# Two adder convolutions: four of nine taps' maxima summed in pairs by accumulating DMA

## The chip, the cores and the metric

The kernel runs on one core of one Trainium2 chip, in one launch. The metric is the device time in microseconds (us) of that core. A core has five engines that run side by side and meet at semaphores: TensorE (PE in the profile; PEld is its weight load), VectorE (DVE), ScalarE (ACT), GpSimd (POOL) and SyncE (SP). Sixteen DMA engines move data when an engine's queue issues a transfer.

## What is computed

The kernel is a chain of four small networks (layers 0 to 3) on one input of 4 images, 128 channels, 64 x 64 pixels, all in float32. The change touches layer 1 alone:

```python
def adder_conv(x, w):            # 3x3, stride 1, pad 1
    # p: [4, 128*9, 4096] patches of x; wf: [128, 128*9]
    # per output channel wc:
    return -jnp.sum(jnp.abs(p - wc[None, :, None]), axis=1)

out = adder_conv(shift_conv(x, w_shift1), w_add1)
out = relu(batchnorm(out, g1, b1))
out = adder_conv(shift_conv(out, w_shift2), w_add2)
out = batchnorm(out, g2, b2)          # then + x and relu
```

`shift_conv` is an ordinary 3x3 convolution whose weights are rounded to powers of two. An adder convolution has no product in it: for every output channel (128), image (4), tap (9), input channel (128) and pixel (4096) it takes |p - w|, and sums over taps and input channels. With 2 adder convolutions that is 2 x 4 x 128 = 1024 pairs of image and output channel; below, one such pair is called a channel.

## The kernel before

Layer 1 calls `shift_adder` twice (tags `a1` and `a2`), and all of the change lies in that function and in the two small loaders `plain` and `normed` of `layer1`. The image after the shift convolution stands in SBUF with a border of zeros as `pb` [128 input channels, 66, 66]; a tap is a shifted view of it. One channel is nine such views of 128 x 4096 elements, each compared with one weight per partition.

Two engines make the absolute values. ACT computes |p - w| directly (L423: ACTIVATE Abs with -w as bias, output tile `aa`). DVE uses |p - w| = 2 max(p, w) - p - w and computes only the maximum (L430: TENSOR_SCALAR, output `da`); the sums of p and of w over the taps that go by maxima are added once, from `sums_of_p` (L370) and `wsum`. PE sums over the 128 input channels: `gather` (L381) multiplies the tile by a 128 x 32 matrix `pick` that is -1 or -2 in column jj and zero elsewhere, so that channel jj's sum lands in row jj of a PSUM bank that collects 32 channels. A tile that PE gathers is called a stream here; it costs 8 matmuls of 128 x 512, and as they are float32 each shows as 2 instructions in the profile, 16 in all.

Before, a channel has eight streams. Taps 4, 5, 6 are Abs on ACT; taps 0 to 3 are maxima on DVE. Taps 7 and 8 share one stream: ACT computes |p - w|/2 of tap 7 (`HALF_TAP`), and DVE adds tap 8's maximum onto that tile (L434: SCALAR_TENSOR_TENSOR), which therefore waits for ACT. So ACT has 4 ACTIVATEs a channel, DVE 4 TENSOR_SCALARs and one SCALAR_TENSOR_TENSOR. In every fourth channel of images 0 to 2 (`extra`) DVE joins tap 3 to tap 2 by a second SCALAR_TENSOR_TENSOR, which takes one stream off PE, and three steps of other PE work are put in: `sums_of_p` and the shift convolution of the next image (L349, with copies to `pb` at L354; its input blocks come by SP's queue, L512 or L519, and their borders are cleared by POOL, L331 to L335). Every 32 channels a bank pair is evacuated (L391, L392) and stored (L394).

The scheduler of the framework orders each engine's instructions by priority; the tile pools set how far an engine may run ahead: `da` has 3 buffers, `aa` 4. POOL has almost nothing to do in this layer, and no DMA is issued from POOL's queue anywhere in the kernel.

Of the kernel before, what the change touches and what calls it, by code (L numbers as in the profile page):

```python
# [28 lines left out]

DVE_TAPS = (0, 1, 2, 3)  # L30
ACT_TAPS = (4, 5, 6)
HALF_TAP = 7
MAX_TAP = 8
# [248 lines left out]
def shift_adder(tc, cm, load, wqs, w_add, stats, y_d, tag):  # L282
# [5 lines left out]

    nc = tc.nc
    NC = P // 32  # L290
    with ExitStack() as ctx:
# [4 lines left out]
        for t, scale in [(HALF_TAP, -0.5)] + [(t, -1.0) for t in ACT_TAPS]:  # L296
            wn[t] = cp.tile([P, P], F32, name=f"{tag}wn{t}")
            nc.vector.tensor_scalar(wn[t], wa[:, t, :], scale, None, ALU.mult)

        pick = {}  # L300
        for v in (-1.0, -2.0):
            pick[v] = cp.tile([P, 63], F32, name=f"{tag}pick{int(-v)}")
            nc.vector.memset(pick[v], 0.0)
            nc.vector.memset(pick[v][:, 31:32], v)

        xin_pool = ctx.enter_context(tc.tile_pool(name=f"{tag}x", bufs=3))
        pb_pool = ctx.enter_context(tc.tile_pool(name=f"{tag}p", bufs=2))
        dp = ctx.enter_context(tc.tile_pool(name=f"{tag}d", bufs=3))
        ap = ctx.enter_context(tc.tile_pool(name=f"{tag}a", bufs=4))
# [6 lines left out]
        sum_taps = DVE_TAPS + (MAX_TAP,)  # L316
        pw = ps_c.tile([P, NC], F32, tag="cv", name=f"{tag}pw")
        for c in range(NC):
            for g in range(4):
                for i, t in enumerate(sum_taps):  # L320
                    nc.tensor.matmul(
                        pw[32 * g : 32 * g + 32, c : c + 1], wa[:, t, 32 * c : 32 * c + 32], cm.one_col,
                        start=(i == 0), stop=(i == len(sum_taps) - 1), skip_group_check=True,
                    )
# [3 lines left out]
        def fetch(b, k):  # L328

            t = xin_pool.tile([P, RB + 2, HP], F32, tag="xin", name=f"{tag}xin{b}_{k}")  # L330
            nc.gpsimd.memset(t[:, :, 0:HP:HP - 1], 0.0)  # L331
            if k == 0:
                nc.gpsimd.memset(t[:, 0, 1 : 1 + W], 0.0)
            if k == NB - 1:
                nc.gpsimd.memset(t[:, RB + 1, 1 : 1 + W], 0.0)  # L335
            lo, hi = max(RB * k - 1, 0), min(RB * (k + 1) + 1, H)
            at = lo - (RB * k - 1)
            load(b, lo, hi, t[:, at : at + hi - lo, 1 : 1 + W])
            return t

        def convolution(b, pb):

            xin = fetch(b, 0)
            for k in range(NB):
                here, xin = xin, fetch(b, k + 1) if k < NB - 1 else None
                pc = ps_c.tile([P, BK], F32, tag="cv", name=f"{tag}pc{b}_{k}")
                for t in range(TAPS):
                    y, x = divmod(t, 3)
                    nc.tensor.matmul(  # L349
                        pc, wqs[:, t, :], here[:, y : y + RB, x : x + W],  # L350
                        start=(t == 0), stop=(t == TAPS - 1),
                    )
                    if t == TAPS - 1:
                        nc.vector.tensor_copy(pb[:, 1 + RB * k : 1 + RB * (k + 1), 1 : 1 + W], rows(pc))  # L354
                    yield

        def padded(b):
            t = pb_pool.tile([P, HP, HP], F32, tag="pb", name=f"{tag}pb{b}")
            clear_border(nc, t)
            return t  # L360

        def sums_of_p(b, pb, sp):

            for k in range(2):
                pc = ps_c.tile([P, BK], F32, tag="cv", name=f"{tag}sp{b}_{k}")
                for i, t in enumerate(sum_taps):
                    y, x = divmod(t, 3)
                    for g in range(4):
                        r = RB * (4 * k + g) + y
                        nc.tensor.matmul(  # L370
                            pc[32 * g : 32 * g + 32, :], cm.ones[:, 0:32], pb[:, r : r + RB, x : x + W],
                            start=(i == 0), stop=(i == len(sum_taps) - 1), skip_group_check=True,
                        )
                    yield
                nc.vector.tensor_copy(sp[:, k, :], pc)

        def gather(pa, jj, v, d, first=False):

            for k in range(2):
                for g in range(4):  # L380
                    nc.tensor.matmul(  # L381
                        pa[k][32 * g : 32 * g + 32, :],
                        pick[v][:, 31 - jj : 63 - jj],
                        d[:, bass.ts(4 * k + g, BK)],
                        start=first, stop=False, skip_group_check=True,
                    )

        def evacuate(b, c, pa, sp):
            for k in range(2):
                o = ep.tile([P, BK], F32, tag="ev", name=f"{tag}ev{b}_{c}_{k}")  # L390
                nc.vector.scalar_tensor_tensor(o, pa[k], wsum[:, c : c + 1], sp[:, k, :], ALU.add, ALU.add)  # L391
                nc.vector.bn_stats(stats[:, c, 2 * b + k, :], o)  # L392
                to = y_d[b, 32 * c : 32 * c + 32, :].rearrange("j (k g w) -> k g j w", k=2, g=4)
                nc.sync.dma_start(to[k], o)  # L394
# [11 lines left out]
        done, late = None, []  # L406
        for b in range(B):
            pb = pb_of[b]

            def view(t):  # L410
                y, x = divmod(t, 3)
                return pb[:, y : y + H, x : x + W]

            sp_of[b] = sp_pool.tile([P, 2, BK], F32, tag="sp", bufs=2, name=f"{tag}sps{b}")
            steps = beside(b, pb_of)
            for co in range(P):
                c, jj = divmod(co, 32)
                name = f"{tag}_{b}_{co}_"

                def absolute(t):  # L420
                    at = ap.tile([P, N], F32, tag="ab", name=f"a{name}{t}")
                    half = t == HALF_TAP
                    nc.scalar.activation(  # L423
                        rows(at), view(t), AF.Abs, bias=wn[t][:, co : co + 1], scale=0.5 if half else 1.0
                    )
                    return at

                def maximum(t):
                    dt = dp.tile([P, N], F32, tag="ad", name=f"d{name}{t}")
                    nc.vector.tensor_scalar(rows(dt), view(t), wa[:, t, co : co + 1], None, ALU.max)  # L430
                    return dt

                def plus_maximum(at, t):
                    nc.vector.scalar_tensor_tensor(  # L434
                        rows(at), view(t), wa[:, t, co : co + 1], rows(at), ALU.max, ALU.add
                    )

                if jj == 0:
                    pa = [
                        ps_a.tile([P, BK], F32, tag=f"pa{k}", name=f"{tag}pa{b}_{c}_{k}") for k in range(2)  # L440
                    ]


                extra = b < B - 1 and co % 4 == 1
                ah = absolute(HALF_TAP)
                d = maximum(DVE_TAPS[0])
                for g in late:
                    gather(*g)
                gather(pa, jj, -2.0, d, first=(jj == 0))
                if done and jj == 0:  # L450
                    evacuate(*done)
                d = maximum(DVE_TAPS[1])
                gather(pa, jj, -2.0, d)
                a = absolute(ACT_TAPS[0])
                gather(pa, jj, -1.0, a)
                a = absolute(ACT_TAPS[1])
                plus_maximum(ah, MAX_TAP)
                gather(pa, jj, -2.0, ah)
                gather(pa, jj, -1.0, a)
                if extra or b == B - 1:  # L460
                    for _ in range(3 if extra else 1):
                        next(steps, None)
                d = maximum(DVE_TAPS[2])
                if extra:
                    plus_maximum(d, DVE_TAPS[3])
                    a = absolute(ACT_TAPS[2])
                    late = [(pa, jj, -1.0, a), (pa, jj, -2.0, d)]
                else:
                    gather(pa, jj, -2.0, d)
                    a = absolute(ACT_TAPS[2])  # L470
                    d = maximum(DVE_TAPS[3])
                    gather(pa, jj, -2.0, d)
                    late = [(pa, jj, -1.0, a)]
                if jj == 31:
                    done = (b, c, pa, sp_of[b])
            for _ in steps:
                pass
        for g in late:
            gather(*g)
        evacuate(*done)  # L480


@with_exitstack
def layer1(ctx, tc, cm, w_shift1, w_add1, g1, b1, w_shift2, w_add2, g2, b2, x1d, y1d, y2d, stats_d):
# [26 lines left out]
    def plain(b, lo, hi, t):  # L511
        nc.sync.dma_start(t, rows(x1d[b])[:, lo:hi, :])  # L512

# [4 lines left out]
    def normed(b, lo, hi, t):  # L518
        nc.sync.dma_start(t, rows(y1d[b])[:, lo:hi, :])  # L519
        nc.vector.tensor_scalar(t, t, mean1, sc1, ALU.subtract, ALU.mult)  # L520
        nc.scalar.activation(t, t, AF.Relu, bias=vec["b1"])
# [867 lines left out]
```

## Time and profile before

| | us |
|---|---|
| median of 3 runs (22255.7 to 22260.05) | 22259.76 |
| the profiled execution, its own time | 22268.93 |
| its span in the trace | 22267.1 |
| adder loop a1, first ACTIVATE to last gather | 2083.8 to 9551.9 |
| adder loop a2, first ACTIVATE to last gather | 9640.3 to 17115.3 |

| in the stretches 2095 to 9540 and 9655 to 17113 (eight windows, 14903 us in sum) | busy us | share |
|---|---|---|
| ACT | 14806.94 | 99% |
| PE | 14385.61 | 97% |
| DVE | 14337.48 | 96% |
| POOL | 28.63 | 0.2% |

The DMA share in these eight windows is 0.01. Outside the loops lie layer 0 (before 2084), the start of a2, and layers 2 and 3 (after 17115); the change does not touch layers 0, 2 and 3.

How to read it: the profile's page gives busy time per engine, a strip of the span in 40 slices, the chain of waits that ended last, and the costliest groups of instructions with their count, busy time and mean duration. Where instructions of one engine overlap slightly (the next begins before the last has ended), the busy time of a group divided by its count is a little under the mean duration.

### The profile page before, as it was taken

The page shows a single profiled execution, that of the slowest core. Times are in us where ns is not written, and L with a number is a line of the kernel's source. Part 1 is how long each engine was busy: PE and PEld are TensorE (multiplying, and loading weights), DVE is VectorE, ACT ScalarE, POOL GpSimd, SP SyncE. Part 2 cuts the span into 40 slices and gives each one's busy share as a digit, 9 for nine tenths or more (in the row PEclk, how much of TensorE's full clock was granted, in tenths as well). Part 3 has the DMA queues.
Part 4 walks back from the last instruction along what each step waited for, and adds up shares of the span by engine and source line. Part 5 has one row for each costly group of instructions (what it writes and reads, how often), then busy time and mean ns, then how long its engine had stood idle before and what let it go on. Part 6 is the DMA issues. An engine that isn't in the chain of part 4 may idle for free.

```text
span 22267.1 us, 326916 instructions
## 1 busy us (share of the span) xinstructions
PE 20221.7 (91%) x144108; PEld 6559.1 (29%) x144108; DVE 19731.7 (89%) x9928; ACT 18549.7 (83%) x9373; POOL 3775.5 (17%) x1774
## 2 busy tenths in 40 slices
PE   9998999999999999999999999999997657688887
PEld 4443222222222232222222222223222222223222
DVE  7887999999999999989999999999998666688887
ACT  5665999999999999989999999999998233556555
POOL 5663000000000000000000000000000000388887
PEclk9999999999999999999999999999998776799998
DMA  0000000000000000000000000000000001588887
GB/s 12 12 5 13 3 4 4 4 4 4 2 4 4 4 2 2 2 8 4 5 3 3 4 3 4 4 2 2 2 3 33 0 0 72 160 217 216 217 219 191
DMA packets 267494, 811.85 MB, mean 36 GB/s; under 512 B 119692, under 2 KB 120596, under 8 KB 195924
## 3 DMA queue, kind: packets, MB, share of 16 engines
q1 hardware_dynamic: 265492, 782.55, 12.8%
q8 instruction: 1127, 18.46, 0.3%
q10 hardware_dynamic: 576, 8.39, 0.1%
q14 instruction: 299, 2.45, 0.0%
HBM read 662.02 MB, written 128.78 MB: 36 GB/s over the span
## 4 chain that ended last, share of the span: by engine, by line
ACT 28%; PE 24%; DVE 23%; issue 16%; DMA 7%; POOL 1%; SPq 0%; DVEq 0%; ACTq 0%; POOLq 0%
ACT aa L423 27%; DVE da L430 11%; PE a1pa L381 5%; PE pe L154 4%; PE pav L197 4%; DMA dl<-delta_d 3%; PE a2pa L381 3%; DVE da L434 3%; DVE aa L434 3%; DMA du<-du_d 2%; DVE h L1043 2%; DVE g L713 1%; PE pd L698 1%; PE mg L1058 1%; POOL dbu L1022 1%
## 5 line engine op out<-in xcount | busy, mean ns | idle before, releaser
L423 ACT ACTIVATE aa<-a1pb,a1wn 128x4096 f32<-128x4096 f32 x2048 | 7411.9, 3711 | 179.0 <-DVE a1pb L354 130.4
L423 ACT ACTIVATE aa<-a2pb,a2wn 128x4096 f32<-128x4096 f32 x2048 | 7410.7, 3709 | 45.3 <-PE a2pa L381 41.5
L430 DVE TENSOR_SCALAR da<-a1pb,a1wa 128x4096 f32<-128x4096 f32 x1952 | 4470.8, 2349 | 0.7 <-PE a1pa L381 0.6
L430 DVE TENSOR_SCALAR da<-a2pb,a2wa 128x4096 f32<-128x4096 f32 x1952 | 4471.0, 2349 | 0.2
L381 PE MATMUL a2pa<-da,a2pick 128*32 128x512 f32 x31232 | 3617.3, 594 | 254.7 <-DVE da L430 252.0
L381 PE MATMUL a1pa<-da,a1pick 128*32 128x512 f32 x31232 | 3615.4, 594 | 253.6 <-DVE da L430 250.9
L381 PE MATMUL a2pa<-aa,a2pick 128*32 128x512 f32 x32768 | 3714.1, 593 | 4.8 <-ACT aa L423 3.3
L381 PE MATMUL a1pa<-aa,a1pick 128*32 128x512 f32 x32768 | 3712.8, 592 | 4.9 <-ACT aa L423 3.3
L434 DVE SCALAR_TENSOR_TENSOR aa<-a1pb,a1wa,aa 128x4096 f32<-128x4096 f32 x512 | 2295.6, 4484 | 281.8 <-ACT aa L423 277.0
L434 DVE SCALAR_TENSOR_TENSOR aa<-a2pb,a2wa,aa 128x4096 f32<-128x4096 f32 x512 | 2295.6, 4484 | 278.2 <-ACT aa L423 274.5
L1058 PE MATMUL mg<-h,ident 128*128 128x512 f32 x4096 | 2017.7, 638 | 421.6 <-ACT m L1067 386.3
L1043 DVE TENSOR_TENSOR_SCAN h<-da,h,dbu 128x1024 f32<-128x1024 f32 x768 | 1804.3, 2349 | 485.6 <-ACT da L1029 393.9
L381 PEld LDWEIGHTS a2pa<-aa,a2pick 128*32 128x32 f32 x32768 | 1068.7, 110 | 2465.4 <-issue 2396.6
L381 PEld LDWEIGHTS a1pa<-aa,a1pick 128*32 128x32 f32 x32768 | 1068.7, 110 | 2463.8 <-issue 2399.3
L381 PEld LDWEIGHTS a2pa<-da,a2pick 128*32 128x32 f32 x31232 | 986.6, 110 | 2707.5 <-issue 2053.9
L381 PEld LDWEIGHTS a1pa<-da,a1pick 128*32 128x32 f32 x31232 | 986.7, 110 | 2705.5 <-issue 2053.7
L1058 PEld LDWEIGHTS mg<-h,ident 128*128 128x128 f32 x4096 | 785.7, 202 | 1658.5 <-issue 809.2
L191 POOL TENSOR_TENSOR ssum<-ssum,et 128x512 f32<-128x512 f32 x960 | 1228.8, 1280 | 233.3 <-ACT et L186 166.4
L1022 POOL TENSOR_TENSOR dbu<-du,B 128x2048 f32<-128x2048 f32 x256 | 1157.2, 4532 | 341.8 <-DMA du<-du_d 267.9
L1071 POOL TENSOR_TENSOR m<-m,C 128x2048 f32<-128x2048 f32 x256 | 1156.1, 4527 | 224.2 <-ACT m L1067 213.4
L1029 ACT ACTIVATE da<-dl,af 128x1024 f32<-128x1024 f32 x512 | 572.9, 1119 | 689.9 <-DMA dl<-delta_d 442.3
L156 ACT COPY et<-pe 128x512 f32<-128x512 f32 x1024 | 596.5, 583 | 591.4 <-PE pe L154 574.8
(273 smaller groups left out, 14087.9 us busy)
## 6 DMA issues: line engine op xcount, KB each, us to landing
dl<-delta_d SPq DMA_DIRECT2D x256, 512.0 KB
dl<-delta_d SPq DMA_DIRECT2D x512, 256.0 KB
du<-du_d SPq DMA_DIRECT2D x256, 512.0 KB
du<-du_d SPq DMA_DIRECT2D x512, 256.0 KB
xs_d<-xs SPq DMA_DIRECT2D x8, 2048.0 KB
sz_d<-sz SPq DMA_DIRECT2D x64, 256.0 KB
delta_d<-dv SPq DMA_DIRECT2D x32, 512.0 KB
du_d<-du SPq DMA_DIRECT2D x32, 512.0 KB
```

The costliest lines, as they stand in the source:

```text
L154: nc.tensor.matmul(pe, k[:, bass.ts(j, P)], unit[u, "q"], start=True, stop=True)
L156: nc.scalar.copy(et, pe)
L191: nc.gpsimd.tensor_tensor(unit[u, "sum"], unit[u, "sum"], at, ALU.add)
L197: nc.tensor.matmul(unit[u, "av"], image[u // NB][2][:, j, :], at, start=(j == 0), stop=(j == NJ - 1))
L381: nc.tensor.matmul(pa[k][32 * g : 32 * g + 32, :], pick[v][:, 31 - jj : 63 - jj], d[:, bass.ts(4 * k + g, BK)], start=first, stop=False, s ...
L423: nc.scalar.activation(rows(at), view(t), AF.Abs, bias=wn[t][:, co : co + 1], scale=0.5 if half else 1.0)
L430: nc.vector.tensor_scalar(rows(dt), view(t), wa[:, t, co : co + 1], None, ALU.max)
L434: nc.vector.scalar_tensor_tensor(rows(at), view(t), wa[:, t, co : co + 1], rows(at), ALU.max, ALU.add)
L1022: then(nc.gpsimd.tensor_tensor(t, du, by_states(tiles[n][0], 0, h), ALU.mult))
L1043: then(nc.vector.tensor_tensor_scan(t[:, cols][:, s], da[:, s], st[n, "dbu", h][:, cols][:, s], 0.0 if e % 4 == 0 else st["last"], ALU.mul ...
L1058: then(nc.tensor.matmul(pm, cm.ident, st[n, way, h][:, bass.ts(k, BK)], start=(way == 0), stop=(way == 1)))
L1071: then(nc.gpsimd.tensor_tensor(m, m, by_states(tiles[n][0], 1, h), ALU.mult))
```

## The change

Taps are dealt out anew, into seven streams. `PAIR_TAPS` ((0,1),(2,3)): DVE computes the maxima of both taps of a pair into two tiles, in halves of 128 x 2048 (`pair`, L455 of the new file), and a DMA issued from POOL's queue adds the first half tile onto the second, SBUF to SBUF (`accum_op=ALU.add`, L457); PE then gathers the sum once. That is four such DMAs of 1 MiB a channel, 4096 in the kernel. Tap 4 is a maximum on DVE (L446), taps 6, 7, 8 are Abs on ACT (L441), and tap 5 (`EITHER_TAP`) is Abs on ACT in even channels and a maximum on DVE in odd ones. The half tiles have 8 buffers (the pairs of one channel), the whole maxima 1, the Abs tiles 3. The combined half-and-maximum stream and the `extra` channels' second SCALAR_TENSOR_TENSOR are gone.

Nearly every instruction of the function is wrapped in `then(...)` (`tc.keep_in_program_order`), so each engine keeps the order in which the code names it: a channel's pairs are gathered one channel later, as the listing shows. The input blocks of a shift convolution are fetched two ahead instead of one, and the normalisation in `normed` is issued when the block is used.

```diff
-DVE_TAPS = (0, 1, 2, 3)
-ACT_TAPS = (4, 5, 6)
-HALF_TAP = 7
-MAX_TAP = 8
+PAIR_TAPS = ((0, 1), (2, 3))
+MAX_TAP = 4
+EITHER_TAP = 5
+ACT_TAPS = (6, 7, 8)
...
-        dp = ctx.enter_context(tc.tile_pool(name=f"{tag}d", bufs=3))
-        ap = ctx.enter_context(tc.tile_pool(name=f"{tag}a", bufs=4))
+        mp = ctx.enter_context(tc.tile_pool(name=f"{tag}m", bufs=8))
+        dp = ctx.enter_context(tc.tile_pool(name=f"{tag}d", bufs=1))
+        ap = ctx.enter_context(tc.tile_pool(name=f"{tag}a", bufs=3))
...
+            ahead = [fetch(b, 0), fetch(b, 1)]
             for k in range(NB):
-                here, xin = xin, fetch(b, k + 1) if k < NB - 1 else None
+                here, landed = ahead.pop(0)
+                landed()
+                if k < NB - 2:
+                    ahead.append(fetch(b, k + 2))
...
+            def absolute(self, i):
+                t = (ACT_TAPS + (EITHER_TAP,))[i]
+                at = ap.tile([P, N], F32, tag="ab", name=f"a{self.name}{t}")
+                then(nc.scalar.activation(rows(at), self.view(t), AF.Abs, bias=wn[t][:, self.co : self.co + 1]))
+                streams[self.n, "abs", i] = (self.jj, self.pa, -1.0, at, (0, 1))
+            def maximum(self, t):
+                dt = dp.tile([P, N], F32, tag="ad", name=f"d{self.name}{t}")
+                then(nc.vector.tensor_scalar(rows(dt), self.view(t), wa[:, t, self.co : self.co + 1], None, ALU.max))
+                streams[self.n, "max", t] = (self.jj, self.pa, -2.0, dt, (0, 1))
+            def pair(self, i, h):
+                ms = []
+                for t in PAIR_TAPS[i]:
+                    mt = mp.tile([P, HL], F32, tag="am", name=f"m{self.name}{t}_{h}")
+                    v = self.view(t, h * H // 2, (h + 1) * H // 2)
+                    then(nc.vector.tensor_scalar(rows(mt), v, wa[:, t, self.co : self.co + 1], None, ALU.max))
+                    ms.append(mt)
+                then(nc.gpsimd.dma_start(ms[1], ms[0], accum_op=ALU.add))
+                streams[self.n, "pair", i, h] = (self.jj, self.pa, -2.0, ms[1], (h,))
...
+            elif co % 2 == 0:
+                summed((n - 1, "pair", 0, 0))
+                ch.absolute(0)
+                ch.pair(0, 0)
+                summed((n - 1, "pair", 0, 1))
+                summed((n - 1, "max", EITHER_TAP))
+                ch.pair(0, 1)
+                ch.absolute(1)
+                summed((n - 1, "abs", 2))
+                ch.maximum(MAX_TAP)
+                summed((n, "abs", 0), first=(jj == 0))
+                summed((n - 1, "pair", 1, 0))
+                ch.absolute(2)
+                ch.pair(1, 0)
+                summed((n - 1, "pair", 1, 1))
+                summed((n, "max", MAX_TAP))
+                summed((n, "abs", 1))
+                ch.pair(1, 1)
+                ch.absolute(3)
...
+            else:
+                summed((n - 1, "pair", 0, 0))
+                ch.pair(0, 0)
+                summed((n - 1, "abs", 2))
+                summed((n - 1, "pair", 0, 1))
+                ch.absolute(0)
+                ch.pair(0, 1)
+                summed((n - 1, "abs", 3))
+                ch.maximum(MAX_TAP)
+                if co % 4 == 1:
+                    for _ in range(3):
                         next(steps, None)
+                ch.absolute(1)
+                summed((n - 1, "pair", 1, 0))
+                ch.pair(1, 0)
+                summed((n, "max", MAX_TAP))
+                summed((n - 1, "pair", 1, 1))
+                ch.absolute(2)
+                summed((n, "abs", 0))
+                ch.pair(1, 1)
+                summed((n, "abs", 1))
+                ch.maximum(EITHER_TAP)
```

Here `n` counts channels over images, `co` is the output channel, `summed(key)` emits PE's gather of that stream (16 instructions, or 8 for a half), and `evacuate` is called once per 32 channels, at the end of an even channel.

## The prediction

> **What bounds the kernel now.** I first read the page's strip of the span, then the groups, then the busy time by windows, and last the order of time on single engines.
>
> The strip shows where the change can matter at all:
>
> ```profile
> PE   9998999999999999999999999999997657688887
> DVE  7887999999999999989999999999998666688887
> ACT  5665999999999999989999999999998233556555
> DMA  0000000000000000000000000000000001588887
> ```
>
> Slices 4 to 31 (557 us each) are the two adder loops: PE, DVE and ACT are all full, DMA and POOL empty. The change takes work off the three full engines and gives it to the empty DMA engines. So the question is the price of the DMA.
>
> Of the three, ACT sets the pace. In the last image, which has no convolution beside it, ACT runs unbroken and DVE waits for it once a channel (columns: start, length, engine and line; the bracket is the idle time before, and who ended it):
>
> ```profile
> 17006.44 36.20 ACT L423 ACTIVATE aa<-a2pb,a2wn 128x4096 f32<-128x4096 f32 x10
> ...
> 17010.17 4.49 DVE L434 SCALAR_TENSOR_TENSOR aa<-a2pb,a2wa,aa 128x4096 f32<-128x4096 f32 x1 [0.91 <-ACT aa L423]
> 17014.58 9.14 DVE L430 TENSOR_SCALAR da<-a2pb,a2wa 128x4096 f32<-128x4096 f32 x4
> 17024.62 4.49 DVE L434 SCALAR_TENSOR_TENSOR aa<-a2pb,a2wa,aa 128x4096 f32<-128x4096 f32 x1 [0.91 <-ACT aa L423]
> ```
>
> The channel's period here is 24.62 - 10.17 = 14.45 us, which is four ACTIVATEs. Over all 1024 channels, by the loop times, (9551.9 - 2083.8 + 17115.3 - 9640.3) / 1024 = **14.59 us**. Everything below is a new period, and the time is 22268.93 + 1024 x (new period - 14.59), against the profiled execution's own time; that stands 9 us, 0.04%, above the median, far less than anything here. (About 0.2% is what a measurement of this kernel can tell from no change.)
>
> **The engines' new shares, per channel.** ACT: 3.5 ACTIVATEs instead of 4. Their spacing back to back is (36.20 - 3.71) / 9 = 3.61 us, so 12.6. PE: seven streams of 16 instructions instead of about eight; 32 instructions stand 3.43 us apart in the timeline (2999 to 3040), 0.107 each, so 7 x 16 x 0.107 = 12.0, plus the convolution in three images of four (18 instructions a block, blocks 7.73 us apart, 8 blocks an image: 62 us / 128 x 0.75 = 0.36) and the sums over p (0.1): 12.5. DVE: eight half maxima and 1.5 whole ones. A half maximum has its exact row in another layer:
>
> ```profile
> L711 DVE TENSOR_SCALAR g<-ht,pww 128x2048 f32<-128x2048 f32 x24 | 30.8, 1284 | 12.3 <-ACT ht L688 12.3
> ```
>
> 1.284 us alone; back to back the overlap of neighbours is 0.085 (four whole ones take 9.14 and not 4 x 2.349, so their spacing is 2.26), so 1.20. 8 x 1.20 + 1.5 x 2.26 = 13.0, and evacuations and copies add 0.1: **13.1**. The SCALAR_TENSOR_TENSORs (4.48 each) go with their wait on ACT. If the DMAs cost nothing, DVE would set 13.1.
>
> The fetch two blocks ahead and the later normalisation I cost at nothing: outside the loop PE's convolution of 144 instructions is one unbroken block of 64.41 us, so it hides the loads already; if it did not, 16 loads of some 3 us would be 50 us, 0.2%. Program order on every engine removes freedom; with PE, ACT and DVE all under 13.1 of the period forecast below, its stalls are covered; uncovered, they fall under the rivals.
>
> **The DMAs.** Four a channel, each adding 128 x 2048 float32 = 1.049 MB onto as much. No row of the trace has an accumulating DMA, an SBUF-to-SBUF one, or one issued by POOL. The nearest rows are the fastest plain copies: after 17140 us the residual's 2 MiB loads keep both queues full (columns: window, length, five engines' busy time, clock, DMA share, GB/s):
>
> ```profile
> 17140.00:17145.00 5.00, 0.00 (x0) 0.00 (x0) 0.00 (x0) 0.00 (x0) 0.00 (x0) 0.50 0.99 410
> 17145.00:17150.00 5.00, 0.00 (x0) 0.00 (x0) 4.74 (x2) 0.00 (x0) 0.00 (x0) 0.50 0.99 426
> 17150.00:17155.00 5.00, 0.00 (x0) 0.00 (x0) 4.96 (x3) 2.69 (x1) 0.00 (x0) 0.50 1.01 433
> 17155.00:17160.00 5.00, 2.07 (x2) 0.50 (x2) 5.00 (x2) 1.89 (x2) 0.00 (x0) 0.50 1.02 436
> 17160.00:17165.00 5.00, 0.00 (x0) 0.00 (x0) 2.14 (x3) 2.65 (x1) 0.00 (x0) 0.50 1.01 433
> ```
>
> At a DMA share of 1 the sixteen engines copy 428 GB/s on average. Lower bound: an accumulation costs what a copy of the same bytes costs, 1.049 / 0.428 = 2.45 us, 9.8 a channel, hidden under DVE's 13.1. Upper bound from these rows: it reads both tiles, so it costs two copies, 4.90 us, **19.6 a channel**, more than any engine. Between them, if reading and writing share one budget, three moves instead of a copy's two: 3.68 us, 14.7, no change. The point that decides is 14.59 / 4 = 3.65 us a DMA, 288 GB/s of results. I take the upper value, since the sum needs two operands fetched for each one stored and 428 is what the engines fetch when full; the work is nearest to two copies. Both ends stay for the range.
>
> The Trainium skill, "Collectives: The Full Stack", in the section on the bandwidth ceiling, says that a reducing DMA is half as fast as a copying one because it reads two sources through one read ring (62 against 32 GB/s measured there). No row here shows it; by it the sum would be the same 19.6 a channel.
>
> A DMA that is the bottleneck must also be kept fed. A half tile's buffers come round once a channel: DMA 4.9, the gather 8 x 0.107 = 0.9, two maxima 2.4, the issue and landing. For the last the nearest row is a small load, issued from 17132.56 and landed at 17135.83: 3.3 us. Sum 11.5, under 19.6, so the other three DMAs cover it. Forecast: period 19.6, 22268.93 + 1024 x (19.62 - 14.59) = 22269 + 5151 = **27420 us**.
>
> **POOL's issue beside DVE.** The new wait is POOL's: its DMA waits for DVE's second maximum, and behind it stand the other DMAs and the border memsets; PE's in-order queue waits for the DMA, and ACT and DVE for PE's buffers. Whether POOL can issue while DVE runs maxima is doubtful:
>
> ```profile
> 3341.45 0.12 POOL L331 MEMSET a1xin<- 128x20 f32 x1 [174.69 <-issue]
> ...
> 3508.57 3.12 POOL L331 MEMSET a1xin<- 128x20 f32 x1 [166.92 <-issue]
> ```
> ```profile
> 3507.01 4.61 DVE L430 TENSOR_SCALAR da<-a1pb,a1wa 128x4096 f32<-128x4096 f32 x2
> 3511.54 0.69 DVE L354 COPY a1pb<-a1pc 128x512 f32<-128x512 f32 x1
> ```
>
> The same memset that takes 0.12 us lasts 3.12 when it starts inside two back-to-back TENSOR_SCALARs: it ends with the second (3511.62), not between the two. DVE's queue is now almost nothing but such instructions. Bounds for the issue: nothing, if writing a DMA's descriptors does not meet what held the memset; or POOL waits until DVE stalls. The Trainium skill, "SBUF — State Buffer", in the box on DVE blocking DMA, says the second: GpSimd cannot write descriptors while DVE runs such an instruction, so the DMA starts late. No row here has a POOL-issued DMA. In the forecast DVE is idle 6.5 of 19.6 us, right where it waits for a buffer, so POOL gets its turns and I add nothing.
>
> **The rivals.**
>
> A. *Copies' price, free issue: faster.* One read's worth of time hides the adding stream: the DMAs take 9.8 and DVE binds at 13.1. 22269 - 1024 x (14.59 - 13.13) = **20774 us**. For it: DMA share 0.01 today. Against: two operands. It decides below 3.28 us a DMA.
>
> B. *POOL locked out, cheap DMA.* DVE runs a channel without a gap, then waits at the reused buffer for issue and landing 3.3, DMA 2.45 and gather 0.9: 13.1 + 6.6 = 19.7, about **27500 us**. For it: the memset row. It looks like the forecast in time, but DMA would be half idle.
>
> C. *Both.* Lockout and two reads: the stall is 3.3 + 4.9 + 0.9 = 9.0, period 22.2, **30020 us**; if DVE and DMA took turns with no overlap at all, 13.1 + 19.6 = 32.7 and 40900.
>
> D. *Middle price.* 3.68 a DMA, or a part of the lockout: period 14 to 18, 21700 to **25800**; at 14.7 it is 22400.
>
> That the change does not do what it says can be set aside: the built program's order has 4096 accumulating DMAs on POOL's queue, four a channel.
>
> **How the numbers follow.** Forecast 0.35 (own range 26300 to 29000), B 0.10, C 0.20, D 0.13, A 0.22. Range: from A's time to C's first, widened slightly, 20600 to 30500; outside lie C's far part (0.13) and little else. Signs: faster is A and a fifth of D, 0.24; within 0.2% 0.01; slower 0.75.
>
> **What would show it.** Forecast right: DMA share near 1 in the loops, a POOL queue that moves 4.29 GB, gaps on DVE at L455 put down to DMA, PE and ACT at two thirds. A: DVE unbroken, DMA half busy. B and C: gaps on DVE with idle DMA engines, and the time between DVE's second maximum and the first packet long. A DMA span under 3.65 us, or a loop still paced by ACT, makes the forecast wrong.

## The result, and the profile after

| | before | after |
|---|---|---|
| median, us | 22257.73 (4 runs, 22245.54 to 22260.05) | 28447.92 (4 runs, 28436.97 to 28449.39) |
| the profiled execution's span | 22267.1 | 28446.1 |
| adder loop a1 | 2083.8 to 9551.9 | 2085.8 to 12626.2 |
| adder loop a2 | 9640.3 to 17115.3 | 12733.1 to 23302.2 |
| period of a channel in the loops | 14.59 | 20.61 |

After / before is 1.2781 (95% interval 1.2759 to 1.2804): the change makes the kernel slower. The forecast was 27420. The period after is (12626.2 - 2085.8 + 23302.2 - 12733.1) / 1024 = 20.61 us, against a forecast of 19.62; 1024 x (20.61 - 14.59) = 6164 us are all but 15 of the 6179 us by which the span grew.

The same strip of the span as before, now in slices of 711 us, with the granted clock and the GB/s that the DMA engines moved:

```profile
PE   9997777777777776777777777777777765668888
DVE  7776666666666666656666666666666666668887
ACT  5656666666666666656666666666666652245565
PEclk9998888888889888888888888888888887769999
DMA  0019999999999999989999999999999980048887
GB/s 14 8 24 205 206 206 207 205 206 206 206 206 205 207 206 207 208 179 205 204 204 207 205 204 205 206 205 205 206 206 207 207 183 0 24 137 217 217 217 198
```

The roles have changed places. In the loops (slices 4 to 33, counted from 1) the three engines that were at 9 are at 6 and 7, and DMA, which was 0, is full. Two windows inside the loop give it in numbers (columns: window, length, busy time of PE, PEld, DVE, ACT, POOL, granted clock, DMA share, GB/s):

```profile
4700.00:7300.00 2600.00, 1882.04 (x14352) 482.34 (x14352) 1690.80 (x1223) 1616.42 (x442) 680.66 (x516) 0.89 1.02 206
7300.00:9900.00 2600.00, 1888.67 (x14340) 483.05 (x14340) 1687.93 (x1222) 1614.78 (x441) 682.42 (x515) 0.89 1.02 206
```

At a DMA share of 1.02 the engines move 206 GB/s. Some 2 of these are other traffic (the loops of the kernel before moved 2 to 4 GB/s), so the price is better read from the count: 4009 such DMAs are issued in the 20650 us of eight windows inside the loops, **5.15 us a DMA**, 20.6 us for a channel's four, and that is the whole period. (The expectations below still take 5.09, which is 1.0486 MB / 0.206.) PE is busy 72%, DVE 65%, ACT 62%. The queue that was not there before, and the shares of the chain of waits that ended last:

```profile
q0 software_dynamic: 589824, 4295.23, 75.1%
```
```profile
DMA 64%; PE 13%; DVE 11%; issue 9%; POOL 2%; ACT 1%; SPq 0%; DVEq 0%; POOLq 0%; ACTq 0%
```

The 4295 MB are 4096 times 1 MiB. Before, ACT led the chain with 28% and DMA had 7%. The groups show who pays (columns: line, engine and operation, output and input, count; busy time, mean ns of one; idle time just before, and what ended most of it):

```profile
L457 POOL DMA_DIRECT2D ma<-ma x4096 | 5515.1, 1347 | 15615.4 <-DVE ma L455 14583.1
L441 ACT ACTIVATE aa<-a1pb,a1wn 128x4096 f32<-128x4096 f32 x1792 | 6565.8, 3712 | 4083.0 <-PE a1pa L407 3949.8
...
L455 DVE TENSOR_SCALAR ma<-a1pb,a1wa 128x2048 f32<-128x2048 f32 x4096 | 5109.6, 1283 | 3667.0 <-DMA ma<-ma 3656.0
```

The half maximum takes 1283 ns, as the forecast had it from another layer (1284). DVE's gaps end with a DMA: the next half tile has to wait for a buffer that an accumulation still reads. ACT's gaps end with PE's gather, which stands in its own order behind a gather that waits for a DMA. The order of time on two engines, DVE first, then POOL (start, length; the bracket is the idle time before, and who ended it):

```profile
14997.95 2.35 DVE L446 TENSOR_SCALAR da<-a2pb,a2wa 128x4096 f32<-128x4096 f32 x1
15000.21 2.47 DVE L455 TENSOR_SCALAR ma<-a2pb,a2wa 128x2048 f32<-128x2048 f32 x2
15005.35 2.48 DVE L455 TENSOR_SCALAR ma<-a2pb,a2wa 128x2048 f32<-128x2048 f32 x2 [2.67 <-DMA ma<-ma]
```
```profile
14998.33 2.09 POOL L457 DMA_DIRECT2D ma<-ma  x1 [5.22 <-DVE ma L455]
15002.98 0.86 POOL L457 DMA_DIRECT2D ma<-ma  x1 [2.56 <-DVE ma L455]
15008.13 2.09 POOL L457 DMA_DIRECT2D ma<-ma  x1 [4.29 <-DVE ma L455]
15013.07 0.86 POOL L457 DMA_DIRECT2D ma<-ma  x1 [2.85 <-DVE ma L455]
```

Issues follow each other at 4.65, 5.15 and 4.94 us, about the pace of the DMA engines. An issue into a pause of DVE takes 0.86 us (15002.98, when DVE has stopped at 15002.68). The one at 14998.33 starts beside DVE's whole maximum and ends 0.12 us after it (15000.42 against 15000.30), while DVE goes on without a gap.

### The profile page after: what moved, and what is told of

The parts are those of the page before. It is cut to its first block, busy times and chain, and to the rows that moved or that the text cites. A ratio compares the mean times of both kernels' runs of the same rounds, so it can differ in the third digit from the quotient of the medians.

```text
span 28446.1 us, 312888 instructions
## 1 busy us (share of the span) xinstructions
PE 21028.5 (74%) x130988; PEld 6174.1 (22%) x130988; DVE 19091.2 (67%) x14544; ACT 16858.0 (59%) x8861; POOL 9269.7 (33%) x5870
## 4 chain that ended last, share of the span: by engine, by line
DMA 64%; PE 13%; DVE 11%; issue 9%; POOL 2%; ACT 1%; SPq 0%; DVEq 0%; POOLq 0%; ACTq 0%
DMA ma<-ma 59%; DVE ma L455 6%; PE pe L153 3%; DMA dl<-delta_d 3%; PE pav L196 3%; DMA du<-du_d 2%; DVE h L1094 1%; PE mg L1109 1%; DVE g L764 1%; PE pd L749 1%; PE a1pa L407 1%; POOL dbu L1073 1%; DVE da L446 0%; DVE x L668 0%; PE a2pa L407 0%
## 5 line engine op out<-in xcount | busy, mean ns | idle before, releaser
L457 POOL DMA_DIRECT2D ma<-ma x4096 | 5515.1, 1347 | 15615.4 <-DVE ma L455 14583.1
L441 ACT ACTIVATE aa<-a1pb,a1wn 128x4096 f32<-128x4096 f32 x1792 | 6565.8, 3712 | 4083.0 <-PE a1pa L407 3949.8
L441 ACT ACTIVATE aa<-a2pb,a2wn 128x4096 f32<-128x4096 f32 x1792 | 6564.9, 3712 | 3698.0 <-PE a2pa L407 3680.0
L455 DVE TENSOR_SCALAR ma<-a2pb,a2wa 128x2048 f32<-128x2048 f32 x4096 | 5107.9, 1283 | 3687.5 <-DMA ma<-ma 3676.0
L455 DVE TENSOR_SCALAR ma<-a1pb,a1wa 128x2048 f32<-128x2048 f32 x4096 | 5109.6, 1283 | 3667.0 <-DMA ma<-ma 3656.0
L407 PE MATMUL a1pa<-ma,a1pick 128*32 128x512 f32 x16384 | 2423.6, 667 | 2141.3 <-DMA ma<-ma 2140.5
L407 PE MATMUL a2pa<-ma,a2pick 128*32 128x512 f32 x16384 | 2401.1, 663 | 1984.2 <-DMA ma<-ma 1982.1
L407 PE MATMUL a1pa<-da,a1pick 128*32 128x512 f32 x12288 | 2033.8, 794 | 770.1 <-DVE da L446 770.1
L407 PE MATMUL a2pa<-da,a2pick 128*32 128x512 f32 x12288 | 2018.9, 789 | 757.2 <-DVE da L446 757.2
L446 DVE TENSOR_SCALAR da<-a2pb,a2wa 128x4096 f32<-128x4096 f32 x768 | 1803.1, 2348 | 0.0
L446 DVE TENSOR_SCALAR da<-a1pb,a1wa 128x4096 f32<-128x4096 f32 x768 | 1803.0, 2348 | 0.0
## 6 DMA issues: line engine op xcount, KB each, us to landing
ma<-ma POOLq DMA_DIRECT2D x4096, 1024.0 KB, 12.8
```

The source lines that it names most:

```text
L407: then(nc.tensor.matmul(pa[k][32 * g : 32 * g + 32, :], pick[v][:, 31 - jj : 63 - jj], d[:, bass.ts(4 * i + g, BK)], start=first, stop=Fal ...
L441: then(nc.scalar.activation(rows(at), self.view(t), AF.Abs, bias=wn[t][:, self.co : self.co + 1]))
L446: then(nc.vector.tensor_scalar(rows(dt), self.view(t), wa[:, t, self.co : self.co + 1], None, ALU.max))
L455: then(nc.vector.tensor_scalar(rows(mt), v, wa[:, t, self.co : self.co + 1], None, ALU.max))
L457: then(nc.gpsimd.dma_start(ms[1], ms[0], accum_op=ALU.add))
```

## The experiments

In the expectations, theory 1 is the price: the DMA engines are full, and nothing that feeds them matters. The others say that they are not fed in time: by POOL's issue beside DVE (theory 2), by the written order (theory 3), or by buffers that come back too late (theory 4, formed after e4). Periods below are (time - 7340) / 1024, where 7340 us is what lies outside the loops.

### Take the accumulation away: e1, e2, e3

One line is edited. e1 deletes it, e2 drops `accum_op`, e3 issues a plain copy from SP's queue:

```diff
-                then(nc.gpsimd.dma_start(ms[1], ms[0], accum_op=ALU.add))
+                then(nc.gpsimd.dma_start(ms[1], ms[0]))        # e2
+                then(nc.sync.dma_start(ms[1], ms[0]))          # e3
```

> The DMA is left out, and PE gathers the second tile of each pair alone, so the first tap of each pair is missing from the sums. If the DMAs' price sets the changed kernel's period of 20.6 us (theory 1), or POOL's late issue does (theory 2), the period falls to DVE's 13.1 us and the time to 7340 + 1024 x 13.1 = 20750 us. If the fixed order of the engines stalls by itself (theory 3), the period stays well above 14 us and the time above 21700 us.

> The same DMA from POOL's queue without the addition: a plain copy, so the first tap of each pair replaces the second in the sums. Theory 1 (an addition costs two transfers, a copy one): about 2.5 us a DMA, 10 a channel, hidden under DVE; period 13.1 to 13.6, 20750 to 21300 us, DMA share about 0.75. Theory 2 (POOL cannot issue beside DVE's maxima): the copy is issued as late as the addition was, 13.1 + 6.6 = 19.7, about 27500 us.

> The same plain copy issued from SP's queue (the first tap of each pair replaces the second in the sums). Theory 1: the same as the copy from POOL, within 1%. Theory 2: 20750 to 21300 us here while the copy from POOL stays near 27500.

Measured, one run each: **20862.08, 21477.1 and 21061.76 us** (before: 22261.7). A window of each, e1, e2 and e3 in this order, columns as above:

```profile
4000.00:5000.00 1000.00, 978.67 (x8671) 294.66 (x8664) 999.28 (x740) 968.22 (x268) 250.61 (x6) 1.00 0.02 4
```
```profile
4000.00:5000.00 1000.00, 944.67 (x8186) 277.34 (x8182) 946.57 (x697) 913.22 (x253) 387.57 (x300) 0.97 0.80 305
```
```profile
4000.00:5000.00 1000.00, 963.60 (x8506) 287.97 (x8502) 982.08 (x725) 947.47 (x262) 22.15 (x6) 1.00 0.81 318
```

Without DMAs, DVE runs 999 of 1000 us and the period is 13.2: the new share of the engines is what the forecast counted (13.1), and the kernel with its taps dealt anew would be 6% faster than before if the sums came for nothing. With copies it would be 4 and 5% faster. At a share of 1 the copies would run at 305 / 0.80 = 381 and 318 / 0.81 = 393 GB/s, 2.75 and 2.67 us a MiB; the other traffic is in these figures too, so read them as about 2.7. So the whole loss hangs on `accum_op`: the same bytes to the same place, issued by the same queue, cost 21477 as copies and 28448 as sums. The difference between e2 and e3, 415 us or 0.4 us a channel, is what POOL as issuer costs when DVE is nearly full and the DMA is cheap (an issue took up to 7.5 us in e2, and 0.46 us in the median on SP in e3). Theory 1 had this at nothing: e2 lies 177 us above its range, and 2% above e3 where within 1% was expected.

### The price by itself: e8

Eight DMAs of 512 KB a channel instead of four of 1 MiB: tiles `[P, HL // 2]`, 16 buffers, `pair` split into two quarters with the view `(2*h+q)*H//4 : (2*h+q+1)*H//4`.

> The changed kernel with the pairs in quarters: eight DMAs of 128 x 1024 a channel, 16 buffers of half the size. If the price goes by bytes, the time stays at 28300 to 28700 us. If each DMA has a fixed part, taken as the 0.19 us by which 5.09 exceeds two copies of 2.45, it is 8 x 2.64 = 21.1 a channel, about 29100 us. If POOL's issue binds, eight issues of 0.9 to 2.1 us a channel make it more than that, over 30000.

Measured, one run: **29384.08 us**.

```profile
3000.00:5000.00 2000.00, 1509.05 (x10532) 378.61 (x10526) 1370.26 (x1644) 1192.65 (x325) 901.36 (x748) 0.94 1.05 197
```

The engines are full again (share 1.05) while DVE has fallen to 69%. The period is 21.53 us, so a DMA of half the size takes 21.53 / 8 = 2.69 us. Two sizes give a line: 0.23 us for each DMA and 4.92 us for each MiB. This is two points for two unknowns, so nothing tests its straightness. 4.92 us a MiB is two transfers at 426 GB/s, and the forecast's rows of plain loads had 428. Of the three expectations, that of a fixed part for each DMA (29100 us) comes nearest.

### What feeds the DMAs: e5, e11

e5 lets sources and destinations rotate in four buffers each; e11 leaves every engine's order to the scheduler:

```diff
-        mp = ctx.enter_context(tc.tile_pool(name=f"{tag}m", bufs=8))
+        mp = ctx.enter_context(tc.tile_pool(name=f"{tag}m", bufs=4))          # e5
-                    mt = mp.tile([P, HL], F32, tag="am", ...)
+                    mt = mp.tile([P, HL], F32, tag="am" + "ab"[len(ms)], ...)  # e5
-    then = tc.keep_in_program_order
+    then = lambda i: i                                                        # e11
...
```

(In e11 the two instructions of the loader in `normed` are freed likewise.)

> The changed kernel with one edit: the source tiles and the destination tiles of the DMAs rotate in two sets of four, so that each buffer is reused exactly one channel later, instead of as soon as the pool has it free (there the last pair of a channel reuses a buffer of that channel's first DMA). Theory 1 (the price of four additions, 5.1 us each, binds): no change, 28300 to 28600 us. Theory 4 (what binds is a buffer that comes round too early, as in the one-pair run): at least 1000 us less.

> The changed kernel with its instructions left to the framework's scheduler instead of fixed in program order; four accumulating DMAs a channel as before. Theory 1 (four DMAs' price): the same within 1%, 28200 to 28700 us. Theory 3 (the fixed order costs time): at least 500 us less.

Measured: e5 **28372.66 us** (4 runs; ratio to before 1.275, interval 1.2731 to 1.2769), e11 **28542.56** (one run). Both within 0.4% of the changed kernel, at 207 GB/s with a share of 1.03 and 204 GB/s with 1.01. The median time from issue to landing moves (12.8 us in the changed kernel, 17.4 in e5, 11.8 in e11), the period does not: more DMAs stand in the queue, and the queue drains at the same pace. Theory 1 holds; that the order or the buffers cost the time falls.

### Half the DMAs: e4, e6

If the price binds, one pair by DMA (two DMAs, 10.3 us a channel) should fit under the engines. In e4 the pair (0,1) goes by DMA, and taps 2 and 3 are gathered singly; e6 also gives the three kinds of half tile (sources, destinations, tiles gathered singly) buffers of their own.

```diff
+                by_dma = i == 0
...
+                    tag, bufs = ("am" + "ab"[len(ms)], (2, 2)[len(ms)]) if by_dma else ("as", 4)  # e6
...
-                then(nc.gpsimd.dma_start(ms[1], ms[0], accum_op=ALU.add))
-                streams[self.n, "pair", i, h] = (self.jj, self.pa, -2.0, ms[1], (h,))
+                if by_dma:
+                    then(nc.gpsimd.dma_start(ms[1], ms[0], accum_op=ALU.add))
+                streams[self.n, "pair", i, h] = [
+                    (self.jj, self.pa, -2.0, m, (h,)) for m in (ms[1:] if by_dma else ms)
+                ]
```

> The full computation with two accumulating DMAs a channel instead of four: pair (0,1) goes by DMA, taps 2 and 3 are gathered as streams of their own, so PE has eight streams. Theory 1: the DMAs take 2 x 5.1 = 10.2 us and are hidden, PE binds at 8 x 1.72 + 0.46 = 14.2 us, 7340 + 1024 x 14.2 = 21900 us, a little faster than before. Theory 2: the stall at the reused buffer stays, period 17 to 22, 24700 us or more.

> The full computation with two accumulating DMAs a channel as in the one-pair run, but with the DMAs' sources, their destinations and the tiles gathered one by one in buffers of their own (2, 2 and 4). Theory 4 for the one-pair run (its stall was a buffer of the channel's own DMA): the stall goes, PE's eight streams bind at 14.2 us, 21900 to 22200 us. Theory 2 (POOL's issue beside DVE): stays above 24500 us.

e4 missed theory 1's 21900 us by far: **26570.22 us** (4 runs, 26556.23 to 26597.57; ratio 1.1933, 1.1913 to 1.1953), with the DMA engines only half busy (share 0.57). The order of time on DVE and POOL (other engines left out), and the view of waits in 3000 to 8000 us (us in total, times, longest), show what DVE waits for:

```profile
5011.80 4.87 DVE L456 TENSOR_SCALAR ma<-a1pb,a1wa 128x2048 f32<-128x2048 f32 x4
...
5014.57 1.02 POOL L460 DMA_DIRECT2D ma<-ma  x1 [15.42 <-DVE ma L456]
...
5016.97 2.09 POOL L460 DMA_DIRECT2D ma<-ma  x1 [1.37 <-DVE ma L456]
...
5023.50 3.68 DVE L456 TENSOR_SCALAR ma<-a1pb,a1wa 128x2048 f32<-128x2048 f32 x3 [4.57 <-DMA ma<-ma]
...
5028.25 6.08 DVE L456 TENSOR_SCALAR ma<-a1pb,a1wa 128x2048 f32<-128x2048 f32 x5 [1.07 <-DMA ma<-ma]
```
```profile
DVE ma L456 <- DMA ma<-ma: 1469.8, 530, 8.0
```

In the built order the pool hands the tiles of the pair (2,3) the buffers of the two DMAs of the *same* channel, issued just before: the half maximum at 5023.50 waits for the DMA issued at 5014.57, and the one at 5028.25 for the DMA of 5016.97. DVE then waits for transfer and landing (9.4 us from the issue in the median) with nothing else to do. e6 takes that reuse away and the time falls to **22758.4 us** (4 runs, 22747.62 to 22792.33; ratio 1.0231, 1.0214 to 1.0248):

```profile
3000.00:5000.00 2000.00, 1944.04 (x17374) 573.25 (x17370) 1779.52 (x1303) 1706.07 (x468) 423.86 (x280) 1.00 0.71 144
```

So theory 4 holds for e4. e6 still missed its expectation by 558 us or more: PE at 97% binds, with eight streams a channel where the changed kernel has seven, at a period of 15.06. The DMA is no longer the bound (0.71), and neither is anything gained.

### Between the two: e7, e9, e10, e12

e7 does three DMAs in even channels and two in odd ones (`by_dma = i == 0 if self.co % 2 else (i, h) != (1, 1)`, buffers 3, 3, 2, and a gather of `pair 1, 0` moved up in the odd channel). e9 and e10 take e6 and spare PE a stream: DVE adds tap 5's maximum onto tap 4's tile, every fourth channel (e9) or every odd one (e10), and tap 4's own gather is left out there:

```diff
+            def join(self, t):
+                then(nc.vector.scalar_tensor_tensor(
+                    rows(dt), self.view(t), wa[:, t, self.co : self.co + 1], rows(dt), ALU.max, ALU.add))
...
-                ch.maximum(EITHER_TAP)
+                (ch.join if joined else ch.maximum)(EITHER_TAP)
```

> The full computation with three accumulating DMAs in even channels and two in odd ones, buffers of their own (3, 3 and 2). DMA 2.5 x 5.1 = 12.75 us, PE 7.75 streams x 1.72 + 0.46 = 13.8 us, DVE 13.1. Theory 1: PE binds, 7340 + 1024 x 13.8 = 21470 us, up to 22000 with stalls of the in-order queues; faster than before. Theory 2: above 24500 us.

> The full computation: one pair by DMA with buffers of their own (the run with one pair that came to 22758 us, PE busy 97%), and in every fourth channel tap 5's maximum is added onto tap 4's tile by a SCALAR_TENSOR_TENSOR on DVE (+2.2 us there), so PE has 7.75 streams instead of 8. If PE is what binds with one pair (theory 1 with the DMA hidden), 0.25 x 1.72 = 0.43 us a channel goes: about 22320 us, near the kernel before. If the DMA still binds through its waits (theory 4), no change: 22700 to 22900 us.

> The same with the joined maximum in every odd channel: PE 7.5 streams (0.86 us a channel less than with 8), DVE 9.6 + 2.26 + 2.2 + 0.1 = 14.2 us. If PE binds with one pair: down to 14.2 to 14.5 a channel, 21900 to 22200 us, slightly faster than before. If the waits on DMAs bind: 22700 us or more.

All three came out slower than theory 1 had them, e7 and e10 inside the other theory's range, e9 outside both: e7 **25431.78 us** (ratio 1.1429, 1.1412 to 1.1446), e9 **24527.52** (1.1022, 1.1006 to 1.1038), e10 **26668.52** (1.1983, 1.1963 to 1.2003), 4 runs each. A window of e7 and one of e10:

```profile
3000.00:5000.00 2000.00, 1714.74 (x14228) 481.52 (x14224) 1500.22 (x1099) 1445.28 (x396) 507.02 (x293) 0.95 0.75 150
```
```profile
3000.00:5000.00 2000.00, 1599.90 (x12986) 437.42 (x12982) 1523.34 (x1030) 1369.83 (x373) 616.77 (x223) 0.91 0.57 114
```

Nothing is full in either: the engines wait for each other. In e10 one such wait can be followed. DVE's order of time, and under it POOL's two issues in 5065 to 5082 us (duration ns min/median/max, first and last start):

```profile
5062.30 4.48 DVE L454 SCALAR_TENSOR_TENSOR da<-a1pb,a1wa,da 128x4096 f32<-128x4096 f32 x1
5066.69 4.88 DVE L467 TENSOR_SCALAR ma<-a1pb,a1wa 128x2048 f32<-128x2048 f32 x4
5071.48 2.35 DVE L447 TENSOR_SCALAR da<-a1pb,a1wa 128x4096 f32<-128x4096 f32 x1
5073.74 4.88 DVE L467 TENSOR_SCALAR ma<-a1pb,a1wa 128x2048 f32<-128x2048 f32 x4
5084.96 1.29 DVE L467 TENSOR_SCALAR ma<-a1pb,a1wa 128x2048 f32<-128x2048 f32 x1 [6.34 <-DMA ma<-ma]
```
```profile
L470 POOL DMA_DIRECT2D ma<-ma x2: 898/5082/9267, 5069.5 to 5078.7; - x2
```

DVE runs without a gap from 5062.30 to 5078.62. POOL begins an issue at 5069.47, and it takes 9.27 us: it ends at 5078.74, when DVE has stopped. The next one takes 0.90. DVE has stopped for want of the buffer that this very DMA reads, and stands for 6.34 us. The mean issue is 2906 ns in e10, 1579 in e6 and 1347 in the changed kernel; (2906 - 1579) x 2 DMAs = 2.7 of the 3.8 us a channel that e10 lies above e6. To test it, e12 is e10 with a copy from SP:

```diff
-                    then(nc.gpsimd.dma_start(ms[1], ms[0], accum_op=ALU.add))
+                    then(nc.sync.dma_start(ms[1], ms[0]))
```

> The kernel of e10 (one pair by DMA, tap 5 joined to tap 4 in every odd channel), but the DMA is a plain copy issued from SP's queue, so the sum of taps 0 and 1 is not made (one tap of the pair is missing). A copy of 1 MiB took 2.67 us in e3, an accumulation 5.09 in the changed kernel. Theory L (e10 loses its time because POOL cannot issue while DVE runs without a gap): SP's issue needs nothing of DVE, the stall goes, and ACT, PE or DVE binds again: 21900 to 22500 us. Theory J (the joins' own waits in the program order cost it, whoever issues): the time stays above 25000. The copy also lands some 2.4 us sooner than the accumulation; two DMAs a channel, this could give back at most 4.9 us a channel, so a fall alone does not part L from a late landing; the gaps of DVE at the pair's tiles and the time from DVE's second maximum to the issue do: in e10 the mean issue was 2906 ns.

Measured, one run: **22819.22 us**, 319 us above theory L's range (DVE is 95% busy in 3000 to 5000 us) and far below theory J's. An issue takes 0.46 us in the median and at most 0.66, and no wait of DVE for a DMA is left in 3000 to 8000 us, where e10 has 253 of them with 921 us. So theory J falls: the joins in their order do not need the time. What takes it is the late end of the DMA; its part from the issue and its part from the transfer (about 2.7 against 5.15 us) are not told apart by e12, since the fall of 3.8 us a channel is less than the 4.9 that the expectation allows to the landing. For e7 and e9 the same cause is likely (issues of up to 8.4 and 9.3 us), but only argued.

No version that computes the whole layer beat the kernel before; the nearest is e6.

## Why the prediction was right

- **The bound now, and where the change acts: right.** Work went from three full engines to idle DMA engines, and the DMA's price decided. e1 to e3 bracket it: no DMA 20862, copies 21062 and 21477, sums 28448.
- **The engines' shares: right.** DVE binds at 13.1 was the forecast without DMAs; e1 has 13.2. PE's 12.5 of 20.6 us at full clock would be 61%; the profile has 72% at a granted clock of 0.89, and 0.72 x 0.89 is 64%. That the clock accounts for most of the difference is an estimate from these two numbers; no run isolates it.
- **The price of the DMA: right in kind, mis-sized.** Of the two bounds, one copy (2.45) and two (4.90), the upper was taken; it is 5.15. Period against period that is 20.61 - 19.62 = 0.99 us a channel, 1014 of the 1028 us by which the forecast was low; the other 14 lie outside the loops or in the rounding. The bytes were priced well (4.92 us a MiB by e8's line); the term that the sum left out is the 0.23 us for each DMA, 0.92 us a channel. Against copies of the same tiles a sum is about 1.9 times as slow. The rule of the Trainium skill ("Collectives: The Full Stack", the bandwidth ceiling: a reducing DMA runs at half the rate of a copying one, for it reads two sources) agrees in the ratio, 206 against 381 to 393 GB/s; the GB/s that it gives, 32 and 62, are those of another transfer and are not seen here.
- **"A half tile's buffers come round once a channel": wrong, without effect here.** In the built order they come round after three DMAs, not four: the half maximum at 15005.35 above starts when the DMA issued at 14992.25 lands, 13.0 us after its issue, and only those of 14998.33 and 15002.98 lie between that one and its own (15008.13). Three DMAs are 15.5 us, still more than the 11.5 of the forecast's sum, and the full DMA engines hide the reuse (e5, with four, is within 0.4%). In e4, where they are half idle, reuse within the channel costs 26570 - 22758 = 3812 us.
- **POOL's issue at nothing: right here, by the reason given.** DVE is idle 35% of the time (forecast 6.5 of 19.6, 33%); issues take 1.02 us in the median and 2.24 at most, and landings follow 12.8 us after the issue in the median (7.0 at least) where a DMA takes 5.15, so as a rule one or two stand in the queue.
- **Rivals.** A's condition (a sum at a copy's price) is the one that failed; its time, 20774, is e1's within 0.5%. B's 6.6 us stall a channel at copies' price is refuted by e2: 0.4 us against SP's queue. The mechanism behind B is real (e10), but not in this kernel, where DVE pauses. C asks for idle DMA engines, and the share is 1.02; its second sum, 32.7 us, comes to some 40800 and not 40900. D's middle price, 3.68 us, is refuted by the 5.15.
- **Program order and fetching ahead at nothing: right.** e11 is within 0.4%, and 7340 us outside the loops stand against 7329 before.

## What to carry to other kernels

A sum by DMA from SBUF to SBUF is no free adder: before moving an addition there, count its results at half of the copy rate (here 4.92 us a MiB and 0.23 us a DMA) against the whole period of the loop, not against the work that it spares. When such a DMA is only just hidden, look next at which buffer waits for its end in the built order, not in the pool's size: reuse within the same channel cost 17% (e4 against e6). And a queue that is full can hide faults in what feeds it, as here the reuse of buffers and the late issues; they come out once it is relieved, so a lighter variant needs its own reading of buffers, order and issues.

## What the runs showed of the hardware

- Accumulating DMAs of 1 MiB keep all 16 engines busy at 206 GB/s (197 at 512 KB), copies between the same tiles would at 381 to 393; some GB/s of other traffic are in each figure.
- POOL beside a DVE without pauses: in e1, where DVE is busy 999 of 1000 us, border memsets, one of which took 0.12 us in the kernel before, last up to 51.5 us. A row of POOL's order of time in e1, and one of DVE's:

```profile
3047.05 51.52 POOL L341 MEMSET a1xin<- 128x20 f32 x1 [114.42 <-PE a1pc L361]
```
```profile
3098.42 0.69 DVE L366 COPY a1pb<-a1pc 128x512 f32<-128x512 f32 x1
```

This memset ends at 3098.57, just after DVE has gone from TENSOR_SCALARs to a COPY (3098.42), as the one in the prediction did (3511.69, with a COPY from 3511.54).

- The Trainium skill ("SBUF — State Buffer", the box on DVE blocking DMA) says that GpSimd cannot write descriptors while DVE runs an instruction in a performance mode that takes two ports; it speaks of one running instruction, and no run here shows the mode of these. Here two behaviours are seen. In the changed kernel the issue waits for the one instruction that runs (2.09 us beside a whole maximum, at 14998.33) and is done 0.12 us later, though DVE leaves no gap there. In e10 it waits out seven, the running one and six more, until DVE stalls (9.27 us). What makes the difference was not found, and stays open.
- The granted TensorE clock is 1.00 in the windows of e1 and e6 shown above, where PE is 97 to 98% busy, and 0.89 in the changed kernel, where it is 72% busy with pauses. The busy share alone does not set it: e8's window has 1509 of 2000 us (75%) at 0.94, e10's 1600 (80%) at 0.91. In the changed kernel PE is not the bound, so the lower clock is not what costs the time.
